# A head's scores over two tiles of keys: one product of 256 columns in place of two of 128

## The chip, the cores and the metric

The kernel runs on one core of a Trainium2 chip. A core has five engines with a queue each: TensorE (PE: matmuls; its weight loads are shown as PEld), VectorE (DVE), ScalarE (ACT), GpSimd (POOL) and SyncE (SP, which here issues DMAs). The metric is the time of one execution on the device, in microseconds; the lower the better. The profile is of one further execution with its own time.

## The reference

A transformer block over 8 sequences of 256 tokens and 256 features, all in fp32: attention with 16 query heads on 4 key and value heads of 128 features, then a mixture of 8 experts (two per token) with a shared expert, each behind a layer norm, with a residual. The part that matters here:

```python
q = _layernorm(q, qn_g, qn_b); k = _layernorm(k, kn_g, kn_b)
q = q * cos + _rotate_half(q) * sin
k = k * cos + _rotate_half(k) * sin
...
scores = jnp.einsum('bhqd,bhkd->bhqk', q, k) / jnp.sqrt(jnp.float32(D))
causal = jnp.triu(jnp.ones((s, s), dtype=bool), k=1)
scores = jnp.where(causal, -jnp.inf, scores)
weights = jax.nn.softmax(scores, axis=-1)
attn = jnp.einsum('bhqk,bhkd->bhqd', weights, v)
```

## The kernel before, in words

Tokens are handled in tiles of 128, so a sequence has two tiles (t = 0 and 1). For each of the 8 sequences, `multiply` (L412) projects a tile onto 512 columns at a time: four groups of query heads, one of key heads, one of values. Queries and keys are normalised (L430 to L456), rotated (L468, L480, L492), turned by TensorE (`turn_heads`, L507) and copied by VectorE with their offset (`settle_heads`, L517) into `qT[g]`, which holds the four heads of group g as 128 features x 256 tokens each, and `kT`, which holds four key heads in the same way. In `kT[:, g, :]` the 256 keys of a head lie side by side.

The attention itself goes by units (L379): for every key head g there are three, (g, 0, 0) with the first tile of queries and all four heads of the group, and (g, 1, 0) and (g, 1, 2) with the second tile of queries and two heads each. That is 12 units a sequence, 96 in all. By causality the first tile of queries needs one tile of keys only, the second both. So each unit has four blocks of 128 x 128 scores, and its PSUM tile `sc` holds 512 fp32 columns: four heads with 128 keys, or two heads with 256 (`shape`, L535). Two buffers of `sc` take turns.

The path of a unit: `score` (L545) makes the products; `masked` (L557, VectorE) adds the causal mask to the last 128 columns of every head; `maximum` (L562, VectorE) and `exponential` (L573, ScalarE) follow; a step later come `inverse` (L581) and `weights` (L588 on GpSimd or L593 on ScalarE); two steps later `turn_weights` (L604, TensorE), `copy_weights` (L609, ScalarE) and `value` (L622, TensorE); then `copy_value` (L633). The output projection `output` (L641, TensorE) runs a sequence behind.

The order is written out by hand. A loop over steps s (L894 to L948) calls, for every step, one part of each kind: step s holds the projection j = s, the turning and settling of projection s - 2, the scores of unit s - 7, the weights' turning of unit s - 9, and some output products of the sequence before. Every engine works through its own instructions in this order. The keys are the first two projections of a sequence, so they are settled in its steps 2 and 3, and the sequence's units are scored in its steps 7 to 18.

Behind the loop come the last outputs, the routing, and the experts' part (L1136 to L1364), where blocks of 128 tokens are gathered by GpSimd's DMAs, multiplied (L1164, L1189), and written back; the shared expert (L284, L304) is put between as filling work.

Of the kernel before, what the change touches and what calls it, by code (L numbers as in the profile page):

```python
# [19 lines left out]
P = 128  # L20
# [28 lines left out]
def block_kernel(  # L49
# [18 lines left out]
    nc = tc.nc  # L68
# [297 lines left out]
    with ExitStack() as actx:  # L366
# [15 lines left out]
        seqs = [{"xnT": {}, "qT": {}, "oT": {}} for _ in range(B)]  # L382
# [152 lines left out]
        def shape(u):  # L535
            return (REP, P) if units[u][1] == 0 else (2, 2 * P)

        def score(b, u):
            g, t, r0 = units[u]
            nh, w = shape(u)  # L540
            sc = ps_sc.tile([P, nh, w], F32, tag="sc", name=f"sc_{b}_{u}")

            for k in range(t + 1):
                for h in range(nh):
                    nc.tensor.matmul(  # L545
                        sc[:, h, k * P : (k + 1) * P],
                        lhsT=seqs[b]["qT"][g][:, r0 + h, t * P : (t + 1) * P],
                        rhs=seqs[b]["kT"][:, g, k * P : (k + 1) * P],
                        start=True,
                        stop=True,  # L550
                    )
            now["sc", b, u] = sc

        def masked(b, u):
# [270 lines left out]
        with tc.manual_schedule():  # L825
# [68 lines left out]
            for s in range(FIRST, LAST):  # L894
# [5 lines left out]
                each(copy_value, u - 3)  # L900
                each(copy_weights, u - 2)
                each(score, u)
                each(normalise, j - 1)
                each(inverse, u - 1)
# [119 lines left out]
    for j in range(2):  # L1024
        h = fc.tile([P, KC * P], F32, name=f"h_{j}")
# [255 lines left out]
    with tc.manual_schedule():  # L1281
# [28 lines left out]
        g, s = G - 3, FULL[G - 3] + 4  # L1310
# [100 lines left out]
```

## Time and profile before

| what | value |
|---|---|
| three runs | 756.83, 759.43, 759.6 us, median 759.43 |
| the profiled execution's own time | 756.9 us |
| its span, from the first to the last instruction | 755.2 us |
| mean granted TensorE clock | 0.988 |
| score products (L545) | 768 matmul and 768 load records, from 32.8 to 551.4 us |

The profile's span is 1.7 us shorter than the execution's own time; the difference lies around it. An fp32 product is recorded as two passes, each with a weight load of its own, so 384 products give 768 records of either kind. Matmuls are pipelined: the next starts before the one before has ended, and the recorded duration of one is a latency. What a matmul costs its engine is therefore read from the distance between the starts of two that follow each other, which the timeline shows. A group row of the profile holds: line, engine, operation, output <- inputs, shapes and count, then busy us and the mean duration in ns of one, then the idle time of the engine just before, and what ended it.

### The profile page before, as it was taken

The page shows a single profiled execution, that of the slowest core. Times are in us where ns is not written, and L with a number is a line of the kernel's source. Part 1 is how long each engine was busy: PE and PEld are TensorE (multiplying, and loading weights), DVE is VectorE, ACT ScalarE, POOL GpSimd, SP SyncE. Part 2 cuts the span into 40 slices and gives each one's busy share as a digit, 9 for nine tenths or more (in the row PEclk, how much of TensorE's full clock was granted, in tenths as well). Part 3 has the DMA queues.
Part 4 walks back from the last instruction along what each step waited for, and adds up shares of the span by engine and source line. Part 5 has one row for each costly group of instructions (what it writes and reads, how often), then busy time and mean ns, then how long its engine had stood idle before and what let it go on. Part 6 is the DMA issues. An engine that isn't in the chain of part 4 may idle for free.

```text
span 755.2 us, 11877 instructions
## 1 busy us (share of the span) xinstructions
PE 721.8 (96%) x3704; PEld 542.3 (72%) x3704; DVE 548.7 (73%) x1467; ACT 459.7 (61%) x1448; POOL 396.8 (53%) x455
## 2 busy tenths in 40 slices
PE   8689999999999999999999999999999899899994
PEld 4356777777777777777777777777887677677773
DVE  5788768788888978887897888678746573364554
ACT  2688877677677767776776777677741333333332
POOL 5667567365555636563664657365212435555423
PEclk9899999999999999999999999999999999999997
DMA  9400000000000000000000000002203133343422
GB/s 309 152 2 1 1 1 7 1 8 1 8 0 8 1 8 8 0 8 1 8 2 8 0 9 8 1 9 79 82 9 91 56 99 119 105 118 108 124 78 76
DMA packets 26917, 32.39 MB, mean 43 GB/s; under 512 B 2980, under 2 KB 23048, under 8 KB 26856
## 3 DMA queue, kind: packets, MB, share of 16 engines
q1 hardware_dynamic: 22752, 21.94, 9.0%
q0 software_dynamic: 3408, 9.31, 4.5%
q8 instruction: 30, 0.49, 0.3%
q10 hardware_dynamic: 696, 0.40, 0.2%
q14 instruction: 31, 0.25, 0.1%
HBM read 22.33 MB, written 9.31 MB: 42 GB/s over the span
## 4 chain that ended last, share of the span: by engine, by line
PE 87%; DVE 4%; ACT 4%; POOL 2%; DMA 2%; issue 1%; POOLq 0%; ACTq 0%; DVEq 0%
PE qkv L412 19%; PE o L641 15%; PE sc L545 11%; PE av L622 10%; PE gu L1164 6%; PE tp L604 5%; PE py L1189 5%; PE gus L284 4%; PE tq L507 4%; PE sd L304 2%; PE xt L1147 1%; PE ht L1179 1%; ACT qn L454 1%; PE in L770 1%; DMA w_qkv<-in_wqkvT 1%
## 5 line engine op out<-in xcount | busy, mean ns | idle before, releaser
L412 PE MATMUL qkv<-w_qkv,xnT 128*128 128x512 f32 x384 | 183.0, 601 | 0.4 <-DVE w_qkv L239 0.4
L480 POOL TENSOR_TENSOR t<-qn,sg_q 128x256 f32<-128x256 f32 x128 | 118.5, 946 | 54.7 <-ACT qn L454 52.9
L445 POOL TENSOR_TENSOR rstds<-ves,nhalf 128x4 f32<-128x4 f32 x80 | 93.6, 1170 | 75.4 <-DVE ves L436 74.9
L641 PE MATMUL o<-wo_sb,oT 128*128 128x256 f32 x512 | 125.1, 384 | 0.0
L454 ACT ACTIVATE qn<-qkv,rstds 128x128 f32<-128x128 f32 x320 | 91.7, 372 | 33.8 <-POOL rstds L445 33.6
L573 ACT ACTIVATE ex<-sc,nmx 128x128 f32<-128x128 f32 (+1 forms) x256 | 105.1, 431 | 5.0 <-DVE nmx L562 4.1
L412 PEld LDWEIGHTS qkv<-w_qkv,xnT 128*128 128x128 f32 x384 | 66.9, 193 | 51.8 <-issue 48.7
L545 PE MATMUL sc<-kT,q 128*128 128x128 f32 x768 | 101.5, 275 | 2.5 <-DVE q L517 2.5
L622 PE MATMUL av<-pT,v 128*128 128x256 f32 (+1 forms) x320 | 98.6, 422 | 0.6 <-ACT pT L609 0.6
L641 PEld LDWEIGHTS o<-wo_sb,oT 128*128 128x128 f32 x512 | 91.4, 190 | 9.3
L545 PEld LDWEIGHTS sc<-kT,q 128*128 128x128 f32 x768 | 93.3, 192 | 2.7 <-ACT w_qkv L247 2.7
L557 DVE TENSOR_TENSOR sc<-sc,mask 128x256 f32<-128x256 f32 (+1 forms) x96 | 49.4, 514 | 44.8 <-PE sc L545 44.4
L507 PEld LDWEIGHTS tq<-ident,t 128*128 128x128 f32 x320 | 40.4, 143 | 47.1 <-issue 35.1
L609 ACT COPY pT<-tp 128x512 f32<-128x512 f32 x96 | 57.2, 596 | 24.2 <-PE tp L604 24.2
L562 DVE TENSOR_REDUCE nmx<-sc 128x2 f32<-128x512 f32 (+1 forms) x96 | 66.2, 690 | 2.8
L604 PEld LDWEIGHTS tp<-ident,ex 128*128 128x128 f32 x384 | 47.6, 141 | 25.7 <-issue 13.2
L622 PEld LDWEIGHTS av<-pT,v 128*128 128x128 f32 x320 | 59.0, 190 | 9.0 <-ACT pT L609 1.0
L468 DVE TENSOR_TENSOR t<-qn,cg_q 128x512 f32<-128x512 f32 x64 | 57.1, 893 | 8.0 <-ACT qn L454 7.6
L430 ACT ACTIVATE sq<-qkv 128x512 f32<-128x512 f32 x80 | 48.3, 603 | 22.9 <-PE qkv L412 13.1
L436 DVE TENSOR_REDUCE ves<-sq 128x4 f32<-128x516 f32 x80 | 54.5, 682 | 7.7 <-ACT sq L430 7.6
L604 PE MATMUL tp<-ident,ex 128*128 128x128 f32 x384 | 58.4, 273 | 1.4 <-DVE xnT L402 0.8
L633 ACT COPY oT<-av 128x512 f32<-128x512 f32 x64 | 37.8, 590 | 35.9 <-PE av L622 35.9
(200 smaller groups left out, 1229.9 us busy)
## 6 DMA issues: line engine op xcount, KB each, us to landing
ys<-yb SPq DMA_DIRECT2D x39, 128.0 KB
w_qkv<-in_wqkvT SPq DMA_DIRECT2D x6, 512.0 KB
x_all<-in_x SPq DMA_DIRECT2D x8, 256.0 KB
wo_sb<-in_woT SPq DMA_DIRECT2D x1, 2048.0 KB
xf_rows<-xf SPq DMA_DIRECT2D x16, 128.0 KB
out<-yo SPq DMA_DIRECT2D x14, 128.0 KB
wgu_sb<-in_wg SPq DMA_DIRECT2D x2, 704.0 KB
wgu_sb<-in_wu SPq DMA_DIRECT2D x2, 704.0 KB
```

The source lines that it names most:

```text
L412: nc.tensor.matmul(ps.rearrange("p h d -> p (h d)"), lhsT=seqs[b]["xnT"][t][:, c, :], rhs=w_qkv[g][:, c, :], start=(c == 0), stop=(c == KC ...
L445: nc.gpsimd.tensor_tensor(rstd, now.pop(("ve", b, j)), nhalf, ALU.pow)
L454: nc.scalar.activation(qn[:, h, :], ps[:, h, :], AF.Copy, scale=rstd[:, h : h + 1])
L480: nc.gpsimd.tensor_tensor(t2[:, :, lo : lo + HD], qn[:, :, hi : hi + HD], sg[s][:, t : t + 1, lo : lo + HD].to_broadcast([P, REP, HD]), AL ...
L507: nc.tensor.transpose(tr[:, h, :], t1[:, h, :], ident)
L545: nc.tensor.matmul(sc[:, h, k * P : (k + 1) * P], lhsT=seqs[b]["qT"][g][:, r0 + h, t * P : (t + 1) * P], rhs=seqs[b]["kT"][:, g, k * P : ( ...
L562: nc.vector.tensor_reduce(out=nm, in_=now["sc", b, u], axis=AX.X, op=ALU.max, negate=True)
L573: nc.scalar.activation(ex[:, h, :], sc[:, h, :], AF.Exp, bias=nm[:, h : h + 1], accum_out=rs[:, h : h + 1],)
L604: nc.tensor.transpose(tr[:, c, :], ex[:, h, k * P : (k + 1) * P], ident)
L609: nc.scalar.copy(pT, now.pop(("tp", b, u)).rearrange("p c q -> p (c q)"))
L622: nc.tensor.matmul(now["av"][:, r0 : r0 + nh, :].rearrange("p h q -> p (h q)"), lhsT=seqs[b]["v"][:, k, g * D : (g + 1) * D], rhs=pT[:, k ...
L641: nc.tensor.matmul(now["o", b, t], lhsT=seqs[b]["oT"][h // REP, t][:, h % REP, :], rhs=wo_sb[:, h, :], start=(h == 0), stop=(h == H - 1),)
```

## The change

`score` no longer splits the keys by tiles. For each head of a unit it makes one product whose moving side is all `w` keys that the unit's queries see: 128 for the first tile of queries, 256 for the second. A unit of the second tile has two products of 256 columns in place of four of 128, which went by tiles of keys first and by heads within them. Units of the first tile have four products of 128 columns as before. Output, inputs and their places in memory stay what they were.

```diff
             sc = ps_sc.tile([P, nh, w], F32, tag="sc", name=f"sc_{b}_{u}")
-
-            for k in range(t + 1):
-                for h in range(nh):
-                    nc.tensor.matmul(
-                        sc[:, h, k * P : (k + 1) * P],
-                        lhsT=seqs[b]["qT"][g][:, r0 + h, t * P : (t + 1) * P],
-                        rhs=seqs[b]["kT"][:, g, k * P : (k + 1) * P],
-                        start=True,
-                        stop=True,
-                    )
+            for h in range(nh):
+                nc.tensor.matmul(
+                    sc[:, h, :],
+                    lhsT=seqs[b]["qT"][g][:, r0 + h, t * P : (t + 1) * P],
+                    rhs=seqs[b]["kT"][:, g, :w],
+                    start=True,
+                    stop=True,
+                )
             now["sc", b, u] = sc
```

## The prediction

> **What bounds the kernel now.** I read the table of engines first, then the chain that ended last, then five stretches of the span, and last the timeline of one stage, because only the timeline tells the pace of the products.
>
> The page's table of engines, its chain by engine, and its rows of the score products and of the other products with 256 columns:
>
> ```profile
> PE 721.8 (96%) x3704; PEld 542.3 (72%) x3704; DVE 548.7 (73%) x1467; ACT 459.7 (61%) x1448; POOL 396.8 (53%) x455
> ...
> PE 87%; DVE 4%; ACT 4%; POOL 2%; DMA 2%; issue 1%; POOLq 0%; ACTq 0%; DVEq 0%
> ...
> L641 PE MATMUL o<-wo_sb,oT 128*128 128x256 f32 x512 | 125.1, 384 | 0.0
> ...
> L545 PE MATMUL sc<-kT,q 128*128 128x128 f32 x768 | 101.5, 275 | 2.5 <-DVE q L517 2.5
> ...
> L545 PEld LDWEIGHTS sc<-kT,q 128*128 128x128 f32 x768 | 93.3, 192 | 2.7 <-ACT w_qkv L247 2.7
> ```
>
> TensorE carries 87% of the chain. [...] The mean of 275 ns is a latency with overlap, not what a pass costs the engine; read as a price it would mislead by a factor of over two, as the timeline below shows.
>
> The stretches (busy us of each engine with its instructions, then the granted clock, DMA share and GB/s):
>
> ```profile
> 0.00:30.00 30.00, 22.00 (x65) 12.96 (x66) 17.07 (x36) 13.04 (x37) 16.35 (x40) 0.84 0.89 290
> 30.00:100.00 70.00, 64.62 (x331) 43.72 (x330) 59.70 (x118) 58.56 (x195) 47.75 (x48) 1.00 0.00 1
> 100.00:550.00 450.00, 450.00 (x2427) 340.49 (x2425) 366.88 (x968) 321.24 (x1032) 247.68 (x268) 1.00 0.04 11
> 550.00:740.00 190.00, 179.82 (x862) 140.92 (x861) 98.88 (x329) 63.55 (x176) 79.23 (x92) 1.00 0.32 93
> 740.00:755.00 15.00, 5.41 (x26) 4.18 (x24) 6.20 (x19) 3.27 (x8) 5.73 (x9) 0.74 0.20 64
> ```
>
> All score products lie between 32.8 and 551.4 us. From 100 to 550 TensorE is busy for 450.00 of 450 us at full clock, and the next engine, VectorE, for 366.88 (82%). Whatever TensorE's queue gets shorter there, the kernel gets shorter.
>
> The timeline of one stage, TensorE's matmuls and then its weight loads (start us, duration, engine, line, and how many):
>
> ```profile
> 301.85 1.46 PE L641 MATMUL o<-wo_sb,oT 128*128 128x256 f32 x6
> 303.15 1.03 PE L622 MATMUL av<-pT,v 128*128 128x256 f32 x4
> 304.01 0.60 PE L604 MATMUL tp<-ident,ex 128*128 128x128 f32 x4
> 304.45 1.06 PE L545 MATMUL sc<-kT,q 128*128 128x128 f32 x8
> 305.34 0.59 PE L412 MATMUL qkv<-w_qkv,xnT 128*128 128x512 f32 x1
> ```
> ```profile
> 304.34 0.97 PEld L545 LDWEIGHTS sc<-kT,q 128*128 128x128 f32 x8
> ```
>
> The starts give the price. Eight score passes take 305.34 - 304.45 = 0.89 us, 111 ns each. Six output passes of 256 columns take 303.15 - 301.85 = 1.30 us, 217 ns each; four value passes of 256 columns take 304.01 - 303.15 = 0.86 us, 215 ns each. Over the whole trace the distances between starts are as even: 95 of the 96 score units take 893 ns for their eight passes (111.6 each), and the median distance at 256 columns is 216 ns at L641, L622, L284, L304 and L1189 alike. Four transposes (L604) take 0.44 us, 109 to 110 each, although their moving side is as wide as a score's: the score's 111.6 is thus a little above what 128 columns need, and its loads, eight beginning at 304.34, come just as close together.
>
> As a check that no wait hides in the "busy" time: between 100 and 550 the counts times these paces are 300 x 429 (L412) + 437 x 216 (L641) + 648 x 111.6 (L545) + 220 x 216 + 54 x 429 (L622) + 630 x 109 (transposes of L604, L507, L674, L400) + 104 x 112 (L770, L681) + 8 x 216 = 450.7 us, against 450. TensorE streams without a gap, so the gain can be only the difference of paces.
>
> **The change part by part.** A unit of the first tile of queries (one tile of keys, four heads) keeps its four products of 128 columns; there are 4 groups x 8 sequences = 32 such units. The other 64 units (two heads, two tiles of keys) had four products, and get two of 256 columns.
>
> *Removed and added on TensorE.* A changed unit had eight passes, 893 ns. It will have four passes of 256 columns. No score pass of that width is in the trace; the nearest rows are L641 and L284, fp32, a 128x128 stationary side, a contiguous 256-column moving side from SBUF, one load per pass: 216. So 4 x 216 = 864 ns, and 893 - 864 = 29 ns a unit; 64 x 29 = **1.9 us**. The bounds: the lowest pace seen at 256 columns is 215, the highest mean at one of these lines 221 (L641, with its late passes in), so the gain lies between 64 x 33 = 2.1 and 64 x 9 = 0.6 us. I take 216, the median of all five lines. The break-even is 893/4 = 223 ns a pass.
>
> *The weight loads.* 256 of 768 loads go, with 192 ns of duration each, 49 us of load time. Here the Trainium skill and the trace part. "TensorE: Matmul & The Clock Gate", Part 3 (the mechanism of packing), says that a load overlaps a running matmul only if it goes to another group of rows; and its section on LDWEIGHTS prices a load of 128 columns at 128/1.2 = 107 ns. Every load here fills all rows, so by that rule each would stand in line, and 256 loads fewer would bring about 27 us (an estimate from that page). "Perfetto Trace Analysis", section on the most contended engine, points the same way: it would have us judge TensorE's headroom by the busy share of its loads, of which 49 of 542 us go. The trace denies both: the scores' loads begin at 304.34 and run on through the products that start from 304.45, and a load with its pass together takes 111.6 ns, so at most 111.6 - 109 = 2.6 ns of it is exposed. The row decides: 1.9 us, not 27.
>
> *Order and waits.* The order on every engine is otherwise the same, no wait is added, and the products are still the same place in the queue. What was k outer and h inner becomes h alone; the fused product needs both tiles of keys at its start, where the first two products needed only the first. That costs nothing: the second tile of keys is settled in step 3 of a sequence (L517), its first reader is unit 1 in step 8, five steps of some 5.4 us later (517 us / 96 units). The one wait of L545 on L517 (2.5 us) is that of the first unit of all. Without that cover it would be one wait per sequence.
>
> *What follows the scores.* The mask (L557) waits for the last product of its unit: DVE sc L557 waits 44.4 us in all for L545, so it follows at once, some 30 ns earlier. The mask, the maximum, the exponential and all their operands are untouched. What is late next: nothing near. VectorE needs 82% of the stretch, ScalarE 71%, GpSimd 55%; TensorE's 450 us become about 448.4.
>
> *Where TensorE isn't saturated.* From 30 to 100 it idles 5.4 us, mostly before 60; some five units of the 96 lie there, three of them changed, 0.1 us of the sum, which may not arrive. Behind 551 no score is left: that part moves earlier as a whole.
>
> The sum: 755.2 - 1.9 = 753.3 us of span, 756.9 - 1.9 = 755.0 for the profiled execution's own time. The other runs of before lie at 756.83, 759.43 and 759.6, with the median 759.43, 2.5 above the profiled one. Against the median the forecast is 759.43 - 1.9 = **757.5 us**, 0.25% less. A measurement of this kernel can tell about 0.5% (3.8 us) from no change, so I expect it within that.
>
> **The rivals.**
>
> *The gain doesn't arrive (no change at all, 759.4).* It would be eaten by a wait on another engine once TensorE is 1.9 us shorter, or by DMA in the last 200 us. For it: 550 to 740 isn't saturated (179.82 of 190), and there the page's chain has DMA links. Against it: not one gap in 450 us, and 18% of room on the next engine. Chance 0.12.
>
> *Slower by the clock.* The granted clock is 0.84 before 30 us and 0.74 after 740: the trace holds half-clock stretches of 3.4, 6.8 and at the end 10 us. At half clock the pace doubles (the 24 transposes of L829 come 213 ns apart, against 109 for the same shape later), so one more stretch of 3.4 us on a busy TensorE costs 1.7 us. Places: the start, with its 5.0 us wait of L507 on L533, and the idle times behind 550, whose lengths shift when everything before is shorter. The decision point is two more stretches: 3.4 - 1.9 = +1.5, 760.9 us; beyond 0.5% needs four, +4.9, 764.3. For it: the runs of before differ by 2.8 us, about what such stretches cost. Against it: nothing in the change adds idle time, and the stretch of the scores is at 1.00 throughout. Chance 0.12, most of it small or with a price of the wide pass above 223 ns.
>
> *More than the sum.* The same stretches can fall away, or a wait at the start or end vanish as things shift: two half-clock stretches fewer give 1.9 + 3.4 = 5.3, 754.1 us. Loads that cost more than the pace shows would do so too, and the row is against them. Chance 0.14.
>
> **How the numbers follow.** The forecast of 1.9 us has 0.62. Of it I give 0.1 to runs that come out beyond 0.5% below, since runs differ by 2.8 us. Faster by over 0.5%: 0.14 + 0.10 = 0.24. Slower by over 0.5%: most of the clock's case, 0.10. Within 0.5%: 0.66. The range: from 756.8 - 1.9 = 754.9, a little further for the case of more, 754.3, to 759.8, which takes in no change at the upper runs.
>
> **What would show it.** L545's line becomes 512 records: 256 of 128 columns at 111 to 112 ns from start to start, 256 of 256 columns at 216, and a changed unit takes 0.86 us where it took 0.89. TensorE's load time falls by some 49 us and its matmul time, by modelled ends, little; between 100 and 550 TensorE still has no idle time, and the last score starts 1.9 us earlier than 551.4. It is wrong if a wide score pass takes over 223 ns, if L545 or L557 shows a new wait, or if the last score comes earlier and the end doesn't.

## The result, and the profile after

| | median | runs |
|---|---|---|
| before | 758.59 us (755.78 to 761.67) | 22 |
| after | 756.31 us (753.52 to 761.52) | 22 |

The ratio is 0.9972, with a 95% interval from 0.9959 to 0.9985: 0.28% less, some 2 us, clear of noise and inside the 0.5% that was called no change beforehand. The median of before moved from 759.43 with three runs to 758.59 with 22; the forecast of 757.5 had been set against the former, and 0.8 of the 1.2 us between it and 756.31 is that move.

The profiled execution is a warning. Its own time is 757.25 us, against 756.9 before: that single pair says slower. The page of after, its table of engines and the rows of the scores:

```profile
PE 722.1 (96%) x3448; PEld 533.7 (71%) x3448; DVE 548.1 (73%) x1467; ACT 459.1 (61%) x1448; POOL 396.7 (53%) x455
...
L543 PE MATMUL sc<-kT,q 128*128 128x256 f32 (+1 forms) x512 | 99.7, 328 | 2.4 <-DVE q L517 2.4
...
L543 PEld LDWEIGHTS sc<-kT,q 128*128 128x128 f32 x512 | 74.7, 191 | 5.9 <-ACT w_qkv L247 2.6
```

256 matmuls and as many loads are gone, and TensorE's busy time is the same: 722.1 us where it was 721.8. Nothing in this view shows a gain. The stretches of after show why the ends agree:

```profile
0.00:30.00 30.00, 21.87 (x64) 12.61 (x65) 15.64 (x34) 13.04 (x37) 15.94 (x39) 0.82 0.89 290
30.00:100.00 70.00, 64.64 (x288) 41.81 (x288) 59.77 (x118) 57.21 (x191) 46.88 (x48) 0.98 0.00 1
100.00:550.00 450.00, 450.00 (x2219) 334.59 (x2218) 368.12 (x970) 322.45 (x1037) 248.85 (x270) 1.00 0.04 11
```

TensorE is still busy for all of 450 us. But the granted clock of the first 30 us is 0.82 (it was 0.84) and that of the next stretch 0.98 (it was 1.00). The first score product starts at 34.6 us, 1.7 later than the 32.9 of before. From the start of the first score unit to that of the last it takes 515.90 us where it took 517.74, 1.84 less. What follows the last unit's start takes 205.0 us, 0.5 more than before. So in this execution the gain is whole in the part that was changed, and a late start and the end hide it.

The timeline of a changed unit, after:

```profile
304.74 0.60 PE L602 MATMUL tp<-ident,ex 128*128 128x128 f32 x4
305.17 1.03 PE L543 MATMUL sc<-kT,q 128*128 128x256 f32 x4
306.04 1.88 PE L412 MATMUL qkv<-w_qkv,xnT 128*128 128x512 f32 x4
307.75 0.60 PE L507 MATMUL tq<-ident,t 128*128 128x128 f32 x4
```

Four passes take 306.04 - 305.17 = 0.87 us, where eight took 0.89. By the starts in the trace, 62 of the 64 changed units take 865 or 866 ns, and the commonest goes 218, 216, 216, 216.

### The profile page after: what moved, and what is told of

Read it like the earlier page. It is cut to its first block, busy times and chain, and to the rows that moved or that the text cites. A ratio compares the mean times of both kernels' runs of the same rounds, so it can differ in the third digit from the quotient of the medians.

```text
span 755.5 us, 11365 instructions
## 1 busy us (share of the span) xinstructions
PE 722.1 (96%) x3448; PEld 533.7 (71%) x3448; DVE 548.1 (73%) x1467; ACT 459.1 (61%) x1448; POOL 396.7 (53%) x455
## 4 chain that ended last, share of the span: by engine, by line
PE 86%; DVE 4%; ACT 4%; issue 2%; DMA 1%; POOL 1%; SPq 0%; DVEq 0%; POOLq 0%; ACTq 0%
PE qkv L412 20%; PE o L639 15%; PE sc L543 10%; PE av L620 10%; PE gu L1162 6%; PE tp L602 5%; PE tq L507 4%; PE py L1187 4%; PE gus L284 4%; PE sd L304 2%; PE xt L1145 1%; ACT qn L454 1%; PE in L768 1%; PE ht L1177 1%; ACT w_qkv L247 1%
## 5 line engine op out<-in xcount | busy, mean ns | idle before, releaser
L412 PE MATMUL qkv<-w_qkv,xnT 128*128 128x512 f32 x384 | 184.4, 606 | 0.0
L412 PEld LDWEIGHTS qkv<-w_qkv,xnT 128*128 128x128 f32 x384 | 72.2, 195 | 55.7 <-issue 51.3
L543 PE MATMUL sc<-kT,q 128*128 128x256 f32 (+1 forms) x512 | 99.7, 328 | 2.4 <-DVE q L517 2.4
L543 PEld LDWEIGHTS sc<-kT,q 128*128 128x128 f32 x512 | 74.7, 191 | 5.9 <-ACT w_qkv L247 2.6
```

The source lines that it names most:

```text
L412: nc.tensor.matmul(ps.rearrange("p h d -> p (h d)"), lhsT=seqs[b]["xnT"][t][:, c, :], rhs=w_qkv[g][:, c, :], start=(c == 0), stop=(c == KC ...
L543: nc.tensor.matmul(sc[:, h, :], lhsT=seqs[b]["qT"][g][:, r0 + h, t * P : (t + 1) * P], rhs=seqs[b]["kT"][:, g, :w], start=True, stop=True,)
```

## The experiments

Eight further runs were made, in two sessions: four edited kernels, then the two kernels of this document again, twice each. The first four share their runs of the kernel before (760.42 us, 59 runs).

**Is it the order?** The change also replaced "tile of keys first" with "head first". This kernel does only that.

```diff
-            for k in range(t + 1):
-                for h in range(nh):
+            for h in range(nh):
+                for k in range(t + 1):
```

> The scores stay four products of 128 columns per unit of the second tile, but in the changed kernel's order: head by head, its two tiles of keys one after the other, the same queries loaded again for the second. Pace theory (the width of a pass decides, a 128-column pass is held by its own load at 111.6 ns): a unit takes 893 ns as before, the time is that of before, ratio 1.000. Rival order (the gain comes from going head by head): 866 ns a unit, some 2 us less, ratio 0.997.

Measured: 760.5 us, ratio 1.000 (0.9986 to 1.0013). Its timeline:

```profile
304.08 1.06 PE L545 MATMUL sc<-kT,q 128*128 128x128 f32 x8
304.97 1.88 PE L412 MATMUL qkv<-w_qkv,xnT 128*128 128x512 f32 x4
```

Eight passes take 0.89 us again, and first to last unit 517.74 us, as before. The order is worth nothing that shows. The run also shows that two products in succession with the same stationary side have four passes with four loads, at full price: the records are 768, and the unit takes 893 ns.

**What holds a narrow pass: its columns or its load?** From the kernel before, the changed units' products are cut in half once more, to 64 columns.

```diff
-            for k in range(t + 1):
+            W = P if t == 0 else P // 2
+            for k in range(w // W):
                 for h in range(nh):
                     nc.tensor.matmul(
-                        sc[:, h, k * P : (k + 1) * P],
+                        sc[:, h, k * W : (k + 1) * W],
...
-                        rhs=seqs[b]["kT"][:, g, k * P : (k + 1) * P],
+                        rhs=seqs[b]["kT"][:, g, k * W : (k + 1) * W],
```

> From the kernel before: the units of the second tile get eight products of 64 columns, sixteen passes with sixteen loads. Pace theory: a pass cannot be shorter than its load, 111.6 ns, so a unit takes 16 x 111.6 = 1.79 us where it took 0.893, and 64 units cost 57 us, about 815 us in all; the next engine, with 82%, has cover for about that much. Rival (a matmul's columns decide, loads are free): 64 columns need half of 109 ns, the unit stays at 0.89 us and the time at that of before.

Measured: 815.35 us, ratio 1.0715 (1.0659 to 1.0772), which is 54 us more (50 to 59, from two runs). The timeline of its matmuls, then of its loads, then its stretch from 100 to 550 us:

```profile
308.20 1.90 PE L546 MATMUL sc<-kT,q 128*128 128x64 f32 x16
309.94 1.94 PE L412 MATMUL qkv<-w_qkv,xnT 128*128 128x512 f32 x4
311.71 0.61 PE L771 MATMUL in<-hot 128*128 128x128 f32 x4
```
```profile
308.10 1.86 PEld L546 LDWEIGHTS sc<-kT,q 128*128 128x128 f32 x16
309.88 0.30 PEld L412 LDWEIGHTS qkv<-w_qkv,xnT 128*128 128x128 f32 x2
```
```profile
100.00:550.00 450.00, 450.00 (x2556) 347.66 (x2555) 334.71 (x867) 292.65 (x937) 221.32 (x251) 1.00 0.01 4
```

Sixteen loads take 309.88 - 308.10 = 1.78 us, 111 ns each, and the products, half as wide, come no faster than that. So some 111.6 ns is the distance of one load from the next, and a pass costs the longer of this and its own columns. The way it is settled is instructive. The first of the sixteen passes takes 58 ns, 64 columns' own time and some 2 ns that the transposes before it leave, and the next fifteen 111 to 112. The load that is still missing is paid by the product behind them: L412's four passes take 311.71 - 309.94 = 1.77 us instead of 1.72, because the first one takes 485 ns instead of 429. Together 1733 + 56 = 1789 ns: sixteen loads of 111.6 ns (1786) and what the transposes left.

A rival is a floor of some 111 ns under every pass, whatever its load. The traces have a place that decides. Among the routing's products are two in bf16, with 8 columns each, and in the trace of before they and their loads follow each other like this:

```profile
313.59 0.17 PE L727 MATMUL rank<-ch,before 128*128 128x8 bf16 x1
313.61 0.17 PE L728 MATMUL rank<-count,ones 128*128 128x8 bf16 x1
313.64 0.46 PE L641 MATMUL o<-wo_sb,oT 128*128 128x256 f32 x1
```
```profile
313.59 0.10 PEld L728 LDWEIGHTS <-ones 128*128 128x128 bf16 x1
313.62 0.30 PEld L641 LDWEIGHTS o<-wo_sb,oT 128*128 128x128 f32 x2
```

By the starts these passes take 28 or 29 and 25 or 26 ns, in all 16 places, and behind L728's load the next one starts after 28 or 29. The fp32 passes of 9 columns (L681) take 111 to 112 from the second on. So neither the pass nor the load has a floor of 111 ns in general; that distance is what an fp32 load of 128 columns takes here.

**The same price, made larger.** Two kernels cut the projections of the changed kernel, 384 passes of 512 columns, into passes of 128 and of 256. The first against the changed kernel:

```diff
-            for c in range(KC):
-                nc.tensor.matmul(
-                    ps.rearrange("p h d -> p (h d)"),
+            for h in range(REP):
+                for c in range(KC):
+                    nc.tensor.matmul(
+                        ps[:, h, :],
...
-                    rhs=w_qkv[g][:, c, :],
+                        rhs=w_qkv[g][:, c, h * D : (h + 1) * D],
```

> From the changed kernel: the projections' products of 512 columns (384 passes of 429 ns) are cut into four of 128 columns, 1536 passes, head by head. This makes the disputed price larger in another place. Pace theory: 1536 x 111.6 - 384 x 429 = +6.7 us against the changed kernel, so about 763 us and a ratio of 1.006 against before. Rival exposed loads (each load costs up to 107 ns more than the pace shows): 1152 loads more would cost some 120 us. Rival free loads (a pass of 128 columns costs its columns alone, a quarter of 429): no difference, ratio 0.997.

The 107 ns are the figure that the prediction takes from the Trainium skill, "TensorE: Matmul & The Clock Gate", section on LDWEIGHTS; from load to load, 111.6 ns were measured.

Measured: 764.4 us, ratio 1.0045 (1.0030 to 1.0059). The second takes two heads at a time; against the first:

```diff
-            for h in range(REP):
+            for h in range(0, REP, 2):
                 for c in range(KC):
                     nc.tensor.matmul(
-                        ps[:, h, :],
+                        ps[:, h : h + 2, :].rearrange("p h d -> p (h d)"),
...
-                        rhs=w_qkv[g][:, c, h * D : (h + 1) * D],
+                        rhs=w_qkv[g][:, c, h * D : (h + 2) * D],
```

> From the changed kernel: the projections' products of 512 columns are cut into two of 256, 768 passes. Pace theory: 768 x 216 - 384 x 429 = +1.2 us against the changed kernel, so 5.5 us less than with products of 128 columns: about 757.5 us, ratio 0.999 against before. Rival exposed loads: 384 loads more cost some 40 us. Rival free loads: no difference between this, the cut into four and the changed kernel.

Measured: 758.79 us, ratio 0.9977 (0.9963 to 0.9992). Between these two lies this document's change, 128 against 256 columns, on three times as many passes: 764.4 - 758.79 = 5.6 us, where the pace theory said 5.5. The timeline at a projection, of the first and then of the second:

```profile
307.40 1.95 PE L413 MATMUL qkv<-w_qkv,xnT 128*128 128x128 f32 x16
309.18 0.60 PE L508 MATMUL tq<-ident,t 128*128 128x128 f32 x4
```
```profile
307.50 1.89 PE L413 MATMUL qkv<-w_qkv,xnT 128*128 128x256 f32 x8
309.23 0.60 PE L508 MATMUL tq<-ident,t 128*128 128x128 f32 x4
```

Sixteen passes take 1.78 us and eight take 1.73, where the uncut four take 307.75 - 306.04 = 1.71. By the starts it is 1784 and 1727 ns against 1717 at most projections, some 67 ns for twelve further loads, so a load that hides behind 128 columns costs its small excess and not its length; 120 us are refuted. Against the changed kernel the sum was a little high for the first: ratios of 1.0045 and 0.9972 differ by 0.73%, 5.5 us, and +6.7 was expected. The trace has 5.2 us more from the first unit to the last (521.14 against 515.90). Seven of the 96 projections lie before the first unit, and 89 x 67 ns are 6.0 us; that the early ones behind it, where TensorE has idle time, bring less is likely, but was not tried by itself.

**What differs between executions of one kernel?** The changed kernel and the one before, twice each, unedited, in the second session, where the one time of before beside them was 754.25 us. Each of the four is a single execution.

> The changed kernel once more, to see what differs between executions of the same kernel. Pace theory: from the first score product to the last it takes 515.9 us again, to 0.1 us; what lies before the first (34.6 us) and behind the last (205.0 us) differs by a microsecond or more, with the length of the half-clock stretches at the start. Rival (the gain in the scores is paid back at the start or the end because of the change): the first score starts at 34.6 us again, and 1.7 us later than before in every profile.

> As the run before it: 515.9 us from the first to the last score product; start and end free to differ by a microsecond or more by the pace theory, as in the first profile of the changed kernel by the rival.

> The kernel before once more. Pace theory: 517.7 us from the first to the last score product; the first score starts anywhere from 32 to 36 us. Rival (the change itself moves the start): it starts at 32.9 us again.

> As the run before it: 517.7 us between the first and last score product, with start and end free to differ by the pace theory; the start at 32.9 us by the rival.

Their times are 750.34 and 749.73 us for the changed kernel, 751.47 and 753.57 for the one before.

| profile | clock, 0 to 30 us | clock, 30 to 45 us | first unit at | first to last unit | last unit to the end |
|---|---|---|---|---|---|
| before | 0.84 | 0.99 | 32.9 | 517.74 | 204.5 |
| before, again 1 | 0.94 | 0.89 | 31.7 | 518.59 | 199.5 |
| before, again 2 | 0.82 | 0.91 | 34.7 | 517.61 | 199.5 |
| after | 0.82 | 0.91 | 34.6 | 515.90 | 205.0 |
| after, again 1 | 0.91 | 0.95 | 33.5 | 515.86 | 199.2 |
| after, again 2 | 0.94 | 0.89 | 31.8 | 516.79 | 199.4 |

The clocks are those of the stretches; the other columns come from the starts in the trace, in us. The stretch from 30 to 45 us in the profile of after, and both first stretches in the second repeat of before:

```profile
30.00:45.00 15.00, 12.19 (x46) 7.00 (x46) 13.19 (x27) 10.04 (x37) 10.88 (x12) 0.91 0.01 2
```
```profile
0.00:30.00 30.00, 21.75 (x64) 12.60 (x65) 15.58 (x34) 13.02 (x37) 15.75 (x39) 0.82 0.88 290
30.00:45.00 15.00, 12.19 (x53) 7.17 (x52) 13.25 (x27) 9.93 (x37) 10.29 (x11) 0.91 0.01 2
```

The same clocks, and the same start of the scores (34.6 and 34.7), with and without the change. The late start is thus not the change's doing: before starts anywhere between 31.7 and 34.7, after between 31.8 and 34.6. The start follows the clock of the first 30 us in the main, though not strictly (32.9 at 0.84, 33.5 at 0.91). The expectation that the distance from first to last unit repeats to 0.1 us failed in one profile of each kernel, by 0.9 us: in both of these the clock records put a half-clock stretch of 3.4 us behind the first unit, at 38.6 and 38.8 us, where the other profiles of the two kernels have none. The stretch from 40 to 45 us in after, again 2, and then in after, has a granted clock of 0.78 and of 1.00:

```profile
40.00:45.00 5.00, 5.00 (x18) 2.92 (x17) 4.37 (x10) 3.48 (x14) 3.90 (x5) 0.78 0.00 0
```
```profile
40.00:45.00 5.00, 4.36 (x19) 3.00 (x20) 3.97 (x11) 4.98 (x22) 4.69 (x6) 1.00 0.02 5
```

Between the profiles with equal clocks in the two stretches of the table, the change is worth 1.72 us (after against before, again 2) and 1.80 us (the other two); the first pair gave 1.84.

## Why the prediction was right

The size and its cause held: 1.9 us were forecast from the paces, 1.7 to 1.8 us were found in the changed part in three pairs of profiles, and 2.3 us between the medians (1.1 to 3.1 by the interval of the ratio).

- *The bound.* Right. TensorE is busy for 450.00 of 450 us after as before, and in the kernel with 64 columns too, so the pace went through: 57 us of work gave 54 us of time (50 to 59). The check of the prediction by counts and paces is added up wrongly, though: its terms come to 448.1 us, not 450.7. The 1.9 us that they lack are as much as the whole gain, but they aren't idle time. Most of it is in 26 passes of L641 behind products of 8 or 9 columns, 83 ns longer than 216 (2.2 us), and in L727 and L728, which were left out (0.7), less the 1.1 us that L681 is under 112 ns, since its first pass takes 31.
- *The pace of the new pass.* The term was 216, taken from L641 and its like. The first wide pass behind the transposes takes 218 or 219, so a unit takes 866 ns and not 864. The sum held, since 2 to 3 ns come back behind it: L412's four passes take 1716 or 1717 ns after most changed units, where they took 1719 or 1720. A narrow pass leaves its excess to the next wide one; before, L412 paid it, now the score does. The prediction had put both terms at nothing; that its sum held is luck in this.
- *The loads.* Rule and row had stood far apart, 27 us against 1.9. The runs decide for the row: 1152 loads more in the projections cost 5 to 6 us. What the Trainium skill says in "TensorE: Matmul & The Clock Gate", Part 3, that a load overlaps only a matmul in another group of rows, doesn't hold for these loads, all of which fill the array. The prediction cites that section by half: its opening also lets a load run ahead if it goes to a background buffer of weights. These traces fit that, but no run here can show the buffer.
- *The load time that goes.* This was mis-sized. 49 us came from 256 x 192 ns, but the loads' durations overlap, with 111.6 ns from one to the next. L545's load time fell by 93.3 - 74.7 = 18.6 us, and that of the engine by 542.3 - 533.7 = 8.6, since loads behind a wide pass no longer overlap with others. No step of the sum rested on it. Of "Perfetto Trace Analysis" the prediction names one measure of headroom; the page names two, the load-busy share and the share of peak arithmetic (MFU), and the load-busy time fell by 1.6% here where the time fell by 0.28%.
- *Order, waits and the other engines.* Right: the order alone gave 1.000, and the row of L543 shows one wait, on the same line as before, of 2.4 us.
- *The sign that was named for the end of the scores.* The last score was to start 1.9 us before 551.4. It started at 551.2. The sign was badly chosen, since it takes in the start, which moves by up to 3 us between executions; the distance from the first unit to the last is the one that tells.
- *The rivals.* That the gain would not arrive has fallen, by the interval of the ratio; so has more than the sum (5.3 us), which lies outside it. The rival of the clock named a mechanism that exists and strikes both kernels alike: by the late start, which goes with the clock in the main, it hid most of the gain in the profiled pair, and it is scatter, not an effect of the change.

No version better than the changed kernel came out of the runs. With loads at 111.6 ns and 128 columns at 109, widening a pass beyond the load's time gains no more per pass than the few nanoseconds seen here.

## What to carry to other kernels

Price a matmul on a saturated TensorE by the distance between starts, and take for each pass the longer of its columns and its load; the mean durations (275 against 384 ns here) promised some 42 us, (2 x 275 - 384) for each of 256 pairs, over twenty times the gain that was there. Joining two products pays much where the halves are narrower than a load takes, 64 columns here, and next to nothing where they already cover it. If an effect is smaller than the scatter of the start, look for it between two marks inside the saturated part, not in the span.

## What the runs showed of the hardware

- The debt of a narrow pass is paid by the next wide one: 3 ns behind passes of 128 columns (432 against 429 at L412), 56 behind those of 64 (485), and 83 behind those of 9 columns (L681 before L641: 299 ns for a pass that otherwise takes 216). In each case it is about 111.6 ns less the narrow pass's own time: 109, 56 (58, less the 2 to 3 ns of the transposes before it) and 28 (31, less the same). The recorded duration of the wide pass is longer by as much: 595 and 648 against 592 ns at L412, 462 against 379 at L641. It may thus be that the record begins before the columns do; the traces don't tell, and for the sum it makes no difference.
- The part behind the last unit's start took 199 us in all four profiles of the second session and 204 to 209 in the six others. Most of it is in the experts' products, where TensorE waits more between 595 and 735 us. In after, then in its first repeat:

```profile
PE gu L1162 <- issue: 3.2, 3, 1.6
PE py L1187 <- ACT hTb L1179: 2.3, 2, 1.8
```
```profile
PE gu L1162 <- issue: 0.6, 2, 0.3
PE py L1187 <- ACT hTb L1179: 0.5, 1, 0.5
```

All of TensorE's waits in that window that the view lists are 7.6 us in after and 2.7 in the repeat, where the whole part differs by 5.8 us. Before has 7.6 us too, and its second repeat 3.1. What causes them in some sessions and not in others wasn't tried and stays open.
